# Held-back additions, a staggered start of v, and weights factored in rounds: a Strassen-Winograd attention kernel for two layers

## The chip, the cores and the metric

The kernel runs on one core of one Trainium2 chip. The metric is the device time of one execution in microseconds. Engines are named as the profile names them: PE (matmul; PEld is its weight load), DVE (vector), ACT (scalar), POOL (GpSimd) and SP (the engine whose queue issues most DMAs).

## The reference

x has the shape [8, 512, 32, 32], all in fp32. Two layers follow each other, both of the same form; 8 groups, 8 heads of 64 channels, S = 1024 tokens per image:

```python
xn  = group_norm(x, groups=8, eps=1e-5) * gamma + beta
q, k, v = Wq @ xn + bq, Wk @ xn + bk, Wv @ xn + bv        # 512 -> 512 each
p   = softmax(q_h^T k_h / sqrt(64))                        # per head h, 1024 x 1024
x   = x + Wo @ concat_h(p v_h) + bo                        # 512 -> 512
```

## The kernel before, in words

**Jobs and stages.** One image in one layer is a job; there are 16, in the order (image 0, layer 0), (1, 0), (0, 1), (1, 1), (2, 0) and so on, in pairs of images. The work alternates between an *attention* of job n and a *phase* n+1, which holds the projections between it and the next attention: V of job n+1, the output projection O of job n, then K and Q of job n+1.

**Attention** (class `Attention`, from L1025) has 64 steps: 8 groups (head pair, half of the queries) of 8 key chunks. A step makes scores on PE (L1046), exp on ACT into a buffer `e` (L1051), and two steps later values on PE (L1097) into `po`. The softmax sums are DVE additions (L1065, L1067), some done by an accumulating DMA of POOL (L1074) and a later addition (L1077). At a group's end ACT copies one half of `po` to `px` (L1118) and DVE adds the other (L1120), the sums are reduced (L1132), gathered by small DMAs of SP, inverted (L1159, L1160) and spread, and q is normalised (L1189). Other small tasks ("chores") are laid at fixed steps of an attention by `put`: the group norm of the next job (its last read-back is the DMA L324, then factors on DVE at L332 to L334, then xn on ACT at L339), sums of xn for the fast multiplication, and the making of weight factors.

**Projections** use the Strassen-Winograd scheme with 7 products for a 2 by 2 block product. K, Q and O are *deep*: two levels, 7 outer chains of 7 inner products, each one matmul of 128x128 on 128x256 (L758). V is one-level in jobs below `DEEP_V` = 3 (L522) and deep from there (L753, 128x128 by 128x128, two matmuls per product). Within a chain the seven products go in a fixed order (1, 5, 6, 2, 7, 3, 4) into PSUM banks named z, y, u, v; ACT copies an intermediate from bank to bank (L466, L470) or to a small buffer `s5` (L785), and the four results are *put*: by ACT (L765, L774, L776) or, for products 7 and 3, by DVE with an addition of `s5` (L781, L783). The seven chain results are then combined by DVE additions of 128x1024 (L797 for K and Q; `plus` at L808 and `add_five` at L803 for V; `more` at L831 for O). `deep_phases` (L602) writes this order: the list `at` interleaves two chains at a time, and for V's first two chains gives an order of its own.

**The order on DVE** is made on the host. Each emitted product advances a model clock; `pump` (L658) takes work from queues by `next_work` (L634): `values` (V's additions), `planned` (the sums that O's products need, with earliest time and due time), `outer` (K's, Q's, O's additions), `extra`. It takes work while DVE's modelled end is less than `AHEAD` = 0.8 us past the clock, and only if the duration (1.22 for an addition, 0.72 for a five-add) fits before the next put's time (`limits`, with `SLACK` = 1.3). An instruction once emitted is executed in that order on its engine.

**The end of an attention.** From job 2's attention on, the first two thunks of V's phase (2 products) are emitted ahead of the last values (`between` in `Attention.run`, L1195), a third between the copies of the two halves of `po` (`middle` in `take`, L1112).

**Weights.** Deep weights lie in device memory, one tile of 7 inner factors per (matrix, layer, outer factor), and are loaded ahead of use through a ring of 6 by SP. They are made on the chip: one-level factors by `first_factors` (L1321) in attentions 0, 1 and 2, in a buffer of tag "deep", stored by `store_factors` (L167); the second level for O, K and Q by `prepare` (L199) in the phase where a matrix is first used, as 28 DVE additions of 128x128 (L159 to L165 through `factor`, L156); for V by `deep_values` (L211) in attentions 2 and 3, in tiles taken from the pool of `e` buffers.

Of the kernel before, what the change touches and what calls it, by code (L numbers as in the profile page):

```python
# [50 lines left out]
AHEAD, TAIL, SLACK = 0.8, 12.0, 1.3  # L51
PLACE = {2: (0, 0), 6: (0, 1), 5: (1, 1), 7: (1, 0)}
DEEP_V = 3
# [25 lines left out]
def fast_path(  # L79
# [87 lines left out]
    def store_factors(w, layer, which):  # L167
        keep = wdram.tile([P, NW, 2, CH], F32, name=f"keep_{which}_{layer}")
        if (which, layer) == (O, 1):
            nc.sync.dma_start(keep, w)  # L170
        else:
            for s in (slice(S1, NW), slice(S3, S3 + 1)):
                nc.sync.dma_start(keep[:, s], w[:, s])
        factors[which, layer] = keep
# [36 lines left out]
    def deep_values(layer):  # L211


        box = {}

        def load(o):
            w = epool.tile([P, NW, P], F32, tag="e", name=f"w_values_{layer}_{o}")
            box[o] = w
            src = (
                raw_block(layer, V, *BLOCK[o]) if o in BLOCK else factors[V, layer][:, FACTOR[o]]  # L220
            )
            nc.sync.dma_start(wide(w), src)

        def make(o):
            w = box.pop(o)
            for part in range(4):
                factor(w, part)
            keep = wdram.tile([P, NW, P], F32, name=f"deep_{V}_{layer}_{o}")
            deep[V, layer, o] = keep
            later(1.0, lambda: nc.sync.dma_start(keep, w))  # L230

        return load, make
# [369 lines left out]
    def deep_phases(n, extra, outs=None, early=()):  # L602
# [11 lines left out]
        began, free_at = [], [0.0]  # L614
# [19 lines left out]
        def next_work(c, forced=False, limit=None):  # L634
            now = clock[0] - began[0] if began else 0.0
            room = 9.9 if limit is None else limit - max(free_at[0], clock[0])
            if planned and planned[0][1] <= now and not forced:
                _, _, _, us, fn = planned.popleft()
            elif values:
                if values[0][0] > room:  # L640
                    return False
# [3 lines left out]
            elif outer:  # L645
                if room < 1.22 and outer[0] not in free:
                    return False
# [14 lines left out]
        def plan_sums():  # L662
            start, combined = out_combines(n - 1, outs)
            c0, c1, c2, c3, c4, c5, c6 = (outs.steps(c) for c in range(7))
            later(0.1, c0[0])
            later(1.0, c0[1])
# [14 lines left out]
        fives = {}  # L681
# [6 lines left out]
        def begin(c):  # L688
# [24 lines left out]
            tiles[which, o] = e  # L713
            s5 = small.tile([P, QT], F32, tag="s5", name=f"s5_{n}_{c}", bufs=3)
# [4 lines left out]
            z, y, u, w = (bank(half, b, f"{b}d_{n}_{c}")[:, :QT] for b in names)  # L719
# [67 lines left out]
        def end(c):  # L787
# [7 lines left out]
            def add(to_, a, b, frees):  # L795
# [3 lines left out]

                outer.append(go)  # L800

            if which == V:
                def add_five():  # L803
                    to_ = p(o)[:, 2:4, :].rearrange("p t (o c) -> p t o c", o=2)
# [3 lines left out]
                def plus(to_, a):  # L808
# [3 lines left out]

                    values.append((1.22, go))

                if c < 2:
                    add_five()
                    spend(0.72)
                else:
                    values.append((0.72, add_five))
# [7 lines left out]
            if which == O:  # L827
# [3 lines left out]
                def more(oh, sh, part, moved=False):  # L831
# [19 lines left out]
                    waiting[oh, sh] += 1  # L851
                    if not moved:
# [78 lines left out]
        if with_v:  # L931
            at[:11] = [
                (0, 0), (0, 1), (0, 2), (0, 3), (0, 4), (1, 0), (0, 5), (1, 1), (0, 6), (1, 2), (1, 3)
            ]
# [90 lines left out]
    class Attention:  # L1025
# [101 lines left out]
        def reduce(self, g):  # L1127
# [63 lines left out]
            times = (0.0, 0.2, 2.0, 4.0) if ends else (0.0, 7.6, 7.7, 16.2)  # L1191
# [3 lines left out]
        def run(self, chores, between=None, middle=None):  # L1195
# [8 lines left out]
            for i in range(3, len(steps) + LEAD):  # L1204
                if i < len(steps):
                    self.scores(i)
                if i - LEAD == len(steps) - 1 and between:
                    between()
# [6 lines left out]
                if kc == NT - 1:  # L1215
                    if middle and g + 1 == len(self.groups):
                        self.reduce(g)
                        self.take(g, middle)
# [101 lines left out]

    def first_factors(put, which_layers):  # L1321

        box = []

        def start():
            box.append(acts.tile([P, 2, NW, 2, CH], F32, tag="deep", name=f"raw_{len(factors)}"))
            for i, (which, layer) in enumerate(which_layers):
                load_blocks(box[0][:, i], layer, which)

        put(2, start)  # L1330
# [543 lines left out]
```

## Time and profile before

| | us |
|---|---|
| median of 4 runs | 3254.39 (3253.22 to 3254.71) |
| the profiled execution | 3253.61 |
| its span | 3251.8 |
| PE busy | 3191.9 |
| DVE busy | 2672.5 |
| ACT busy | 2054.8 |
| POOL busy | 279.7 |

The profiled execution's own time is 1.8 us more than its span. The granted TensorE clock was 0.998. Stages, as they stand in the trace from the first matmul of one to the first matmul of the next:

| stage | us | stage | us |
|---|---|---|---|
| attention 0 | 110.12 | phase 1 | 92.46 |
| attention 1 | 110.03 | phase 2 | 92.91 |
| attention 2 | 116.45 | phase 3 | 96.16 |
| attention 3 | 112.20 | phase 4 | 91.19 |
| attention 4 and most later ones | 109.17 | most later phases | 90.6 |

A stage's length is read against that of a later stage with the same matmuls: attentions all have the same, phases 3 and later too (phases 1 and 2 have the one-level V). Idle time on an engine other than PE has a price only where PE waits for it in the end.

### The profile page before, as it was taken

To read this page: it belongs to the slowest core of one execution; us is meant where nothing else is said; L and a number is where in the kernel's file an instruction comes from. 1 tells how busy PE (TensorE), PEld (TensorE's weight loads), DVE (VectorE), ACT (ScalarE), POOL (GpSimd) and SP (SyncE) were. 2 spreads that over 40 slices of the span, in tenths; PEclk is the share of its full clock that TensorE was granted. 3 is DMA by queue.
4 is the path that set the end of the run, shared out by engine and by line. 5 is a ranking of instruction groups with operands and counts; after the bars stand their busy time and mean duration, and the time that the engine had idled before them with its cause. 6 is when DMAs were issued, how large, how long until landed. Compare 5 with 4: busy or idle time off the path is not lost.

```text
span 3251.8 us, 61327 instructions
## 1 busy us (share of the span) xinstructions
PE 3191.9 (98%) x24009; PEld 1862.2 (57%) x24009; DVE 2672.5 (82%) x3952; ACT 2054.8 (63%) x3583; POOL 279.7 (9%) x318
## 2 busy tenths in 40 slices
PE   9999999999999999999999999999999999999998
PEld 7365483563846638365483754737557374573844
DVE  8796897979879788796987969789697896978957
ACT  4746656566666666666666666666666666666663
POOL 0100001001010010100001000010000100001000
PEclk9999999999999999999999999999999999999999
DMA  7555556667635354455554535446455463544733
GB/s 270 139 148 135 148 178 152 179 171 182 203 73 147 104 143 129 86 160 141 138 174 93 166 86 134 119 93 187 121 134 173 90 196 61 139 113 98 212 85 78
DMA packets 188810, 453.47 MB, mean 139 GB/s; under 512 B 38120, under 2 KB 56160, under 8 KB 188256
## 3 DMA queue, kind: packets, MB, share of 16 engines
q1 hardware_dynamic: 139664, 300.04, 27.9%
q0 software_dynamic: 48848, 149.44, 25.1%
q8 instruction: 190, 3.11, 0.4%
q14 instruction: 108, 0.88, 0.1%
HBM read 246.69 MB, written 52.10 MB: 92 GB/s over the span
## 4 chain that ended last, share of the span: by engine, by line
PE 82%; DVE 11%; DMA 4%; issue 2%; ACT 1%; SPq 0%; POOL 0%; DVEq 0%; ACTq 0%; POOLq 0%
PE sc L1046 25%; PE po L1097 25%; PE zd L758 8%; PE vd L758 8%; PE yd L758 3%; PE vd L753 3%; PE ud L758 3%; PE zd L753 3%; DVE acc L1067 1%; PE ud L753 1%; PE yd L753 1%; DMA x<-p 1%; DMA w<-deep 1%; DVE k L797 1%; PE z L522 1%
## 5 line engine op out<-in xcount | busy, mean ns | idle before, releaser
L1051 ACT ACTIVATE e<-sc 128x1024 f32<-128x1024 f32 x1024 | 1043.0, 1023 | 574.0 <-PE sc L1046 521.0
L1046 PE MATMUL sc<-q,k 64*64 64x512 f32 x8192 | 1059.4, 590 | 8.7 <-ACT e L1051 8.4
L1097 PE MATMUL po<-e,v 64*64 64x512 f32 x8192 | 1061.0, 590 | 0.0
L1046 PEld LDWEIGHTS sc<-q,k 64*64 64x64 f32 x8192 | 311.0, 133 | 574.0 <-issue 514.1
L1097 PEld LDWEIGHTS po<-e,v 64*64 64x64 f32 x8192 | 312.0, 133 | 560.9 <-issue 546.0
L1067 DVE TENSOR_TENSOR acc<-acc,e 128x1024 f32<-128x1024 f32 x320 | 389.2, 1216 | 49.9 <-ACT e L1051 41.7
L1074 POOL DMA_DIRECT2D e<-e x224 | 192.2, 858 | 1749.3 <-ACT e L1051 1272.0
L1065 DVE TENSOR_TENSOR acc<-e,e 128x1024 f32<-128x1024 f32 x128 | 156.3, 1221 | 202.4 <-ACT e L1051 202.3
L1077 DVE TENSOR_TENSOR acc<-acc,e 128x1024 f32<-128x1024 f32 x224 | 272.1, 1215 | 1.9
L758 PE MATMUL zd<-deep,w 128*128 128x256 f32 x860 | 245.0, 384 | 22.7 <-DVE p L783 20.7
L758 PE MATMUL vd<-deep,w 128*128 128x256 f32 x804 | 224.5, 380 | 3.4 <-ACT yd L466 1.6
L758 PEld LDWEIGHTS zd<-deep,w 128*128 128x128 f32 x860 | 159.0, 190 | 59.0 <-DVE p L783 31.5
L758 PEld LDWEIGHTS vd<-deep,w 128*128 128x128 f32 x804 | 152.2, 190 | 26.4 <-ACT yd L466 2.0
L1132 DVE TRANSPOSE_TENSOR_REDUCE r<-acc 128x32 f32<-128x1024 f32 x128 | 159.4, 1245 | 4.3
L839 POOL DMA_DIRECT2D x<-p x61 | 72.9, 1195 | 1003.0 <-ACT p L774 621.3
L785 ACT COPY s<-vd 128x256 f32<-128x256 f32 x195 | 72.6, 372 | 114.7 <-PE vd L758 63.4
L785 ACT COPY s<-zd 128x256 f32<-128x256 f32 x209 | 77.8, 372 | 102.3 <-PE zd L758 57.9
L1120 DVE TENSOR_TENSOR q<-po,px 128x512 f32<-128x512 f32 x115 | 78.3, 681 | 49.0 <-ACT px L1118 48.9
L470 ACT COPY ud<-vd 128x256 f32<-128x256 f32 x209 | 75.2, 360 | 64.7 <-PE vd L758 53.5
L470 ACT COPY ud<-zd 128x256 f32<-128x256 f32 x195 | 71.0, 364 | 70.5 <-PE zd L758 43.2
L753 PE MATMUL vd<-w,deep 128*128 128x128 f32 x780 | 113.1, 278 | 0.0
L758 PE MATMUL vd<-os,w 128*128 128x256 f32 x368 | 109.6, 387 | 2.1 <-DVE p L783 0.6
(308 smaller groups left out, 4717.4 us busy)
## 6 DMA issues: line engine op xcount, KB each, us to landing
w<-deep SPq DMA_DIRECT2D x378, 448.0 KB, 5.5
e<-e POOLq DMA_DIRECT2D x224, 512.0 KB, 4.7
x<-p POOLq DMA_DIRECT2D x61, 512.0 KB, 7.6
rb<-rd SPq DMA_DIRECT2D x96, 256.0 KB, 4.0
deep<-w SPq DMA_DIRECT2D x42, 448.0 KB, 3.6
x<-x_dram SPq DMA_DIRECT2D x28, 512.0 KB, 3.7
out_dram<-x SPq DMA_DIRECT2D x28, 512.0 KB, 3.2
w<-keep SPq DMA_DIRECT2D x32, 256.0 KB, 4.8
```

Source lines behind the costliest of these rows:

```text
L470: nc.scalar.copy(u, z)
L753: nc.tensor.matmul(ps[:, tokens], moving[i][:, tokens], lhs[:, FACTOR[i], :], start=(start and ti == 0), stop=True, skip_group_check=True,)
L758: nc.tensor.matmul(ps, lhs[:, FACTOR[i], :], moving[i], start=start, stop=True, skip_group_check=True,)
L785: return chain(product, lambda ps: nc.scalar.copy(s5, ps), put, z, y, u, w)
L1046: nc.tensor.matmul(sc[h * HD : (h + 1) * HD, j, :], k[r, hp, k0 : k0 + HD], q[r, hp, sh * HALF : (sh + 1) * HALF], start=True, stop=True,)
L1051: nc.scalar.activation(e, sc, AF.Exp, scale=SCALE)
L1065: nc.vector.tensor_add(acc[g], self.es[i - 1], e)
L1067: nc.vector.tensor_add(acc[g], acc[g], e)
L1074: nc.gpsimd.dma_start(self.summed[i], self.summed.pop(i - 1), accum_op=ALU.add)
L1077: nc.vector.tensor_add(self.acc[g], self.acc[g], self.summed.pop(i))
L1097: nc.tensor.matmul(po[g][j * HD : (j + 1) * HD, h, :], v[r, kc, d0 : d0 + HD], e[r, j, :], start=(kc == 0), stop=(kc == NT - 1),)
L1132: nc.vector.tensor_reduce(self.r[:, 0, m, :], self.acc.pop(g).rearrange("p j (b e) -> p (j b) e", e=RP), AX.X, ALU.add, apply_transpose=True,)
```

## The change

**Additions are queued later.** Each addition gets a time before which the planner does not take it: the model clock at the end of the product chain that makes its last term, plus `BEHIND` = 1.2 us. It holds for K, Q, O and V alike. V's five-adds, which free an `s5`, are forced when two more chains have begun.

**V's start.** The last values of an attention come first, then the copy px, V's first product, and the copy py; V's first two chains are interleaved product by product from their third product on. The PSUM banks of a chain are allocated in the order y, u, v, z whatever their use. The first sums for O are emitted at 6.2 and 6.9 us instead of 0.1 and 1.0, the spread of the last group's inverse 5.6 us later than before and its normalisation 4.2 us later.

**Weights.** V is deep from job 2. `first_factors` and `deep_values` go. `deep_round` makes both levels of one matrix in one buffer [128, 7, 7, 128]: 4 loads of 256 KB, 4 DVE additions of 128x512, 4 of 128x896, and one store of 3136 KB. Two rounds run in each of attentions 0 and 1 (from steps 2 and 25), one in attentions 2 and 3; they use the same buffer tag one after the other. Layer 0's K and Q stay as before. The deep steps of attention 1 are put at steps 49 to 58, and layer 1's output bias is made in phase 2 from the queue `ahead`.

```diff
-AHEAD, TAIL, SLACK = 0.8, 12.0, 1.3
+AHEAD, TAIL, SLACK, BEHIND = 0.8, 12.0, 1.3, 1.2
-DEEP_V = 3
+DEEP_V = 2
+ROUNDS = {0: ((O, 0), (K, 1)), 1: ((V, 1), (Q, 1)), 2: ((O, 1),), 3: ((V, 0),)}
...
+    def deep_round(which, layer):
+        box = []
+        def start():
+            t = acts.tile([P, NW, NW, P], F32, tag="deep", name=f"round_{which}_{layer}")
+            box.append(t)
+            for i in range(2):
+                for j in range(2):
+                    nc.sync.dma_start(
+                        t[:, 2 * j + i, 0:4, :].rearrange("p (cc h) o -> p cc (h o)", cc=2),
+                        raw_block(layer, which, i, j),
+                    )
+        def outer_(part):
+            factor(box[0][:, :, 0:4, :], part)
...
+        def inner(part):
+            factor(box[0].rearrange("p f a o -> p a f o"), part)
+        def store():
+            keep = wdram.tile([P, NW, NW, P], F32, name=f"deep_{which}_{layer}")
+            nc.sync.dma_start(keep, box[0])
...
         def next_work(c, forced=False, limit=None):
             now = clock[0] - began[0] if began else 0.0
-            room = 9.9 if limit is None else limit - max(free_at[0], clock[0])
+            start = max(free_at[0], clock[0])
+            room = 9.9 if limit is None else limit - start
+            if forced:
+                start = 1e9
...
-                if values[0][0] > room:
+                if values[0][0] > room or ready[values[0][1]] > start:
                     return False
...
-                if room < 1.22 and outer[0] not in free:
+                if outer[0] not in free and (room < 1.22 or ready.get(outer[0], 0.0) > start):
                     return False
...
-            later(0.1, c0[0])
-            later(1.0, c0[1])
+            later(6.2, c0[0])
+            later(6.9, c0[1])
...
+            while unread and unread[0] <= c - 3:
+                next_work(c, True)
...
-            z, y, u, w = (bank(half, b, f"{b}d_{n}_{c}")[:, :QT] for b in names)
+            taken = {b: bank(half, b, f"{b}d_{n}_{c}")[:, :QT] for b in sorted(names, key="yuvz".index)}
+            z, y, u, w = (taken[b] for b in names)
...
+                ready[go] = clock[0] + BEHIND
                 outer.append(go)
...
-                (0, 0), (0, 1), (0, 2), (0, 3), (0, 4), (1, 0), (0, 5), (1, 1), (0, 6), (1, 2), (1, 3)
+                (0, 0), (0, 1), (1, 0), (0, 2), (1, 1), (0, 3), (1, 2), (0, 4), (0, 5), (1, 3), (0, 6)
...
-            times = (0.0, 0.2, 2.0, 4.0) if ends else (0.0, 7.6, 7.7, 16.2)
+            times = (0.0, 0.2, 7.6, 8.2) if ends else (0.0, 7.6, 7.7, 16.2)
...
-                if i - LEAD == len(steps) - 1 and between:
-                    between()
                 self.values(i - LEAD)
...
-                    if middle and g + 1 == len(self.groups):
+                    if taken and g + 1 == len(self.groups):
                         self.reduce(g)
-                        self.take(g, middle)
...
-                if n == 0:
-                    first_factors(put, [(O, 0), (V, 1)])
-                elif n == 1:
-                    first_factors(put, [(K, 1), (Q, 1)])
-                elif n == 2:
-                    first_factors(put, [(O, 1)])
+                for at, made in zip((2, 25), ROUNDS.get(n, ())):
+                    first, *made, store = deep_round(*made)
+                    put(at, first)
+                    for i, fn in enumerate(made):
+                        put(at + 4 + i, fn)
+                    put(at + 12, store)
...
+                    late = (49, 50, 51, 53, 54, 55, 57, 58)
+                    for at, fn in zip(late if n == 1 else (41, 43, 45, 47, 49, 51, 53, 55), deep_first):
...
-                if DEEP_V - 1 <= n <= DEEP_V:
-                    load, make = deep_values(jobs[n + 1][1])
-                    for i, o in enumerate(OUTER_V):
-                        put(23 + 4 * i, lambda o=o: load(o))
-                        put(29 + 4 * i, lambda o=o: make(o))
...
-                att.run(chores, between, both[2])
+                att.run(chores, True)
                 extra = ahead
                 plan_sums()
-                banks(1, "one")
+                banks(0, "one")
                 if n + 2 < len(jobs):
                     reads, steps = norm_steps(n + 2)
-                for thunk in both[3:]:
+                att.take(len(att.groups) - 1, both[0])
+                banks(1, "one")
+                for thunk in both[1:]:
                     thunk()
```

## Prediction

> **What bounds the kernel.** I read the page's busy line first, then the slices, the costliest groups, a table of windows by stage, the waits, and then the timeline around each wait.
>
> ```profile
> span 3251.8 us, 61327 instructions
> PE 3191.9 (98%) x24009; PEld 1862.2 (57%) x24009; DVE 2672.5 (82%) x3952; ACT 2054.8 (63%) x3583; POOL 279.7 (9%) x318
> ```
>
> PE is busy 98% of the span at a granted clock of 0.998, so a change can win in two ways only: fewer or shorter matmuls, and fewer gaps between them. The windows (columns: stretch, its us, busy time and count of PE, PEld, DVE, ACT, POOL, clock, DMA share, GB/s) say where the gaps are. They are attention 1, attention 2, phase 3, attention 3, a steady phase and a steady attention:
>
> ```profile
> 285.00:395.00 110.00, 110.00 (x1025) 38.97 (x1024) 86.73 (x107) 73.00 (x76) 12.63 (x15) 1.00 0.59 138
> 490.00:604.00 114.00, 108.74 (x1000) 37.82 (x992) 93.72 (x134) 71.31 (x75) 12.78 (x15) 0.99 0.67 173
> 604.00:700.50 96.50, 90.27 (x506) 76.99 (x498) 80.90 (x151) 57.60 (x156) 5.99 (x5) 1.00 0.64 195
> 700.50:812.50 112.00, 109.43 (x1017) 38.56 (x1016) 94.65 (x137) 73.17 (x76) 12.61 (x15) 1.00 0.62 150
> 1013.00:1104.00 91.00, 89.31 (x506) 77.59 (x506) 76.56 (x125) 57.49 (x157) 4.77 (x4) 1.00 0.47 137
> 1104.00:1212.70 108.70, 108.70 (x1016) 38.55 (x1008) 88.65 (x109) 73.16 (x76) 12.62 (x15) 1.00 0.49 107
> ```
>
> Measured from first matmul to first matmul in the trace, a steady attention lasts 109.17 us and a steady phase 90.60; but attention 2 lasts 116.45 (7.3 more), attention 3 112.20 (3.0 more) and phase 3 96.16 (5.6 more). Phases 1 and 2 last 92.46 and 92.91. The rest repeats at 199.8 us per job, and its loss sits in the phase, where matmul starts 0.2156 us apart (128x256) and 0.1113 (128x128) would make 86.1 us, 4.5 less than the 90.6.
>
> **The change, part by part.** All sums are against the profiled run, 3253.61 us (span 3251.8, 1.8 around it); the median of the runs, 3254.39, is 0.8 above it.
>
> *1. Attention 2, V's weights.* There ACT's exp waits for the store of a small weight tile, since those tiles are taken from the buffers that exp writes, and PE waits in turn:
>
> ```profile
> PE sc L1046 <- ACT e L1051: 5.3, 2, 3.7
> ACT e L1051 <- DMA deep<-w_values: 9.4, 2, 5.7
> ```
>
> The change makes V's factors in a buffer of their own (the tag "deep", free in early attentions). These two waits end, and the restarts after them; of the 7.3 us about 1 may remain, since DVE is the busiest here (93.7 of 114): **-6.5** (bounds -7.3 and -5, the latter if DVE is late next). Attention 3 likewise: **-2.7** of 3.0 (bounds -3.0 and -1).
>
> *2. Prepares out of the phases.* In phase 1 (O, layer 0), 2 (K, Q, layer 1) and 3 (O, layer 1) DVE makes each product's inner factors between the adds: 28 instructions of 128x128 per matrix at 282 to 292 ns, 8.0 us each. DVE's puts and adds are what PE waits for in phase 3 (five waits of 0.4 to 0.8 us on L783 or L781, three of 0.4 to 1.4 on ACT's copy L470, one of 0.7 on a load). Without them phase 3 becomes a steady phase: -5.6, and -0.4 for part of what 4 gains: **-6.0** (bounds -7 and -4). In phase 1 DVE is 67.7 of 81 us busy and V stays one-level: its stalls are only 4.9 us over the spacing, and I take the prepares' part, **-1.8** (bounds -3 and 0). Phase 2 gets the deep V: 196 matmuls at 0.1113 are 21.8 us in place of 112 at 0.2156, 24.1, so -2.3; and of its 5.4 us of stalls some 0.6 go: **-2.9** (bounds -4 and -1).
>
> *3. The rounds' price, attentions 0 and 1.* A round adds, on DVE, four 128x512 (0.68 each) and four 128x896 instructions (not in the trace; between 128x768 at 0.95 and 128x1024 at 1.22, so 1.08): 7 us, 14 for two, less 5.3 of removed factors. DVE goes from 86.7 to about 100 of 110 in attention 1, which also takes the deep steps of V: full, not over. What weighs more is SP's queue. The round's result leaves as one store of 3136 KB, and the second round's first load waits at SP's head for it, with everything behind it. In attention 1 that is the group norm's read-back:
>
> ```profile
> 307.63 1.86 SPq L324 DMA_DIRECT2D mr<-dg  x2
> 318.87 0.15 DVE L332 TENSOR_TENSOR mul<-mr,vec_sb 128x4 f32<-128x4 f32 x1
> 324.96 1.23 ACT L339 ACTIVATE xn<-x,off,mul 128x1024 f32<-128x1024 f32 x1
> ```
>
> Before, mr is issued at 307.63, lands 6.4 us later, and ACT uses it at 324.96 with nothing to wait for. After, the store is issued near 311.5. Its duration isn't in the trace: the tile view of the existing factor stores gives 7.4 us for 1792 KB, which by size makes 12.9, an upper end; the fastest slice of the DMA view (463 GB/s) makes 7, the lower. I take 12.9, since the 1792 KB store is the nearest row. Then mr is issued near 325, lands near 330, and ACT, which has exp of later scores queued behind xn, stands about 6 us; scores run less than one step (1.72) ahead, so PE loses some 5 to 6, and DVE's wait for mr delays the sums whose buffers exp needs: **+6** (at 7 us for the store 0, at 12.9 with DVE pushed over its slack 12). This row speaks against the change. The Trainium skill, "DMA: Bandwidth & Descriptors", section on the anatomy of one DMA, fits a DMA as 2.0 us plus bytes over 436 GB/s, 9.4 us by estimate here; with it the wait would be about 2.5 instead of 6. "Perfetto Trace Analysis", section DMA Optimizations, says that splitting DMAs may let some start sooner: a rule against the single store, which no row of before can test. In attention 0 the same block delays a gather by some 4 us; DVE has 110.5 - 85.9 = 25 us of room, less the 9 added: **+1** (bounds 0 and 3).
>
> *4. Steady phases, 12 of them (4 to 15).* (a) V's start: two products begin ahead of attention's last values.
>
> ```profile
> 1212.94 0.71 PE L753 MATMUL vd<-w,xn 128*128 128x128 f32 x4
> 1214.03 1.09 PE L1097 MATMUL po<-e,v 64*64 64x512 f32 x8
> 1215.05 0.71 PE L753 MATMUL vd<-w,deep 128*128 128x128 f32 x4
> 1215.19 0.59 ACT L1118 COPY px<-po 128x512 f32<-128x512 f32 x1 [0.68 <-PE po L1097]
> ```
>
> PE changes tile shape three times; I count some 1.0 us over the spacing here, of which 0.3 (one change) must stay. The change puts the values first and lets two products alternate after them. ACT must then do px, py (0.59 each) and the products' copies (0.36) within the first products; walking ACT's copies at these durations against matmuls at 0.1113 leaves about 0.1 of stalls beside the one change of shape, since the first products use the banks (v, z) that are free early: 0.4 in place of 1.0, **-0.6** (ends -0.7 and, if the crowd on ACT holds PE for a whole px, 0). (b) Inside V, the product's third buffer (s5, three of them) waits for a five-add that is queued behind other adds; 0.15 to 0.7 plus 0.26 per phase. The forced service two products later takes about **-0.3**. (c) K's and Q's ends. This is the page's dearest idle of a phase, 20.7 us in all, two of 0.79 per phase:
>
> ```profile
> L758 PE MATMUL zd<-deep,w 128*128 128x256 f32 x860 | 245.0, 384 | 22.7 <-DVE p L783 20.7
> ...
> 1076.27 2.49 DVE L797 TENSOR_TENSOR k<-k 128x1024 f32<-128x1024 f32 x2 [0.84 <-ACT k L774]
> 1078.68 0.48 DVE L783 SCALAR_TENSOR_TENSOR p<-zd,bias_step,s 128x256 f32<-128x256 f32 x1
> 1079.21 0.70 PE L758 MATMUL zd<-deep,w 128*128 128x256 f32 x2 [0.79 <-DVE p L783]
> ```
>
> The first add was queued 0.84 before its term was there; two adds (2.49) then make the put 1.5 late where about 0.5 is free, so PE waits (0.97 with the restart). The change holds an add back for 1.2 us after its product's last step. At Q's end the adds then come behind the put: -1.07. At K's end one add lies between the puts of the next product and pushes by about 1.4: -0.1 only. In O the held-back adds meet the sums' blocks of four (1.5 us) and the puts are later there: +1.3 by my walk through the order of DVE's instructions. (c) is **+0.1**, with -2 and +2.5 as ends. Per phase -0.6 - 0.3 + 0.1 = -0.8; twelve make **-9.6** (ends -24 and +20).
>
> Sum: -6.5 - 2.7 - 6.0 - 1.8 - 2.9 + 6 + 1 - 9.6 = -22.5, so **3231 us**.
>
> **Rivals.** *A: waits only change places.* (c) plus ACT's crowded start of V cancel (a) and (b): 12 x 0.8 = 9.6 given back, 3241. For it: ACT and DVE serve PE step by step with 0.5 us of slack. *B: both ends' gaps vanish*, with no loss in O: 12 x 1.2 less again, about 3217. For it: the cause of each 0.79 gap is an add queued too early. Against it: the K end, where the window between two puts (3.0 us) holds the later adds too. *C: slower.* The held-back adds bunch: where three adds (3 x 1.14 to 1.22, 3.4 to 3.7) fall between two puts 3.0 us apart, of which the puts themselves take 0.8 and about 0.5 is free, the put is late by 0.7 to 1.0 and by more at the next. With the early gains standing (-13), it decides from +1.1 us per phase over 12; at +2 it gives 3253.6 - 13 + 24 = 3265. Against it: DVE is 76.6 of 91 us busy in a phase, so backlogs drain. *D: SP blocked worse.* The stores cost 12 in attention 1 and 3 in attention 0 instead of 7: 3239. *E: staged weights aren't there in time*, so that phases 1 and 2 wait for their first loads; unlikely, as the stores land 60 us ahead.
>
> **How the numbers follow.** Forecast (3224 to 3236) 0.40, A and D together 0.27, B 0.17, C 0.10, E or another way of no gain 0.06. A measurement of this kernel can tell about 0.2%, 6.5 us, from no change. Faster by more than that: forecast, B and nearly all of A and D, 0.83; within it 0.08; slower 0.09. The range leaves out C and the last of B and E: 3212 to 3249, narrower than the ends of 4 alone since those twelve phases can't all be at an end without a whole window of adds going wrong.
>
> **What the changed profile would show.** Right: in attentions 2 and 3 no wait of exp on a store, lengths near 109.5; phase 3 near 91; one gap near 0.8 per phase on L783's counterpart instead of two; no values among V's first matmuls; in attention 1 ACT's xn waiting for DVE's factors near 40 us into it, PE's scores for exp behind it, 5 us or so. Wrong: a phase as long as 90.6 or longer (A, C); the 0.8 gaps all gone (B); attention 1 longer than 116 (D) or 110 (store faster than its row says).

## The result, and the profile after

The changed kernel takes 3258.68 us (median of 40 runs, 3253.55 to 3267.81) beside 3254.56 us for the kernel before (60 runs): ratio 1.0013, 95% interval 1.0009 to 1.0018. It is 4 us slower than before; the forecast was 3231, in a range of 3212 to 3249. The profiled execution took 3260.8 us. First the top of its page:

```profile
span 3259.0 us, 61423 instructions
PE 3187.3 (98%) x24093; PEld 1861.8 (57%) x24093; DVE 2662.0 (82%) x3822; ACT 2093.7 (64%) x3623; POOL 280.6 (9%) x318
```

PE is busy 4.6 us less than before and the span is 7.2 longer: the waits grew. The stages, from first matmul to first matmul, say where. (Before, from attention 2 on, two of V's products and the last values stood in each other's stage; to compare like with like, 0.86 us, eight of the values' matmul records, is moved there from the phase to the attention.)

| stage | before | after | difference |
|---|---|---|---|
| up to attention 0 | 82.47 | 83.22 | +0.8 |
| attention 0 | 110.12 | 117.63 | +7.5 |
| phase 1 | 92.46 | 88.62 | -3.8 |
| attention 1 | 110.03 | 128.73 | +18.7 |
| phase 2 | 92.91 | 88.09 | -4.8 |
| attention 2 | 117.31 | 122.22 | +4.9 |
| phase 3 | 95.30 | 88.30 | -7.0 |
| attention 3 | 113.06 | 120.25 | +7.2 |
| phase 4 | 90.33 | 89.69 | -0.6 |
| attention 4 to phase 15 | 2203.25 | 2190.61 | -12.6 |
| the rest | 144.56 | 141.64 | -2.9 |

So every phase gained, all but phase 4 (0.6 for 0.8) more than forecast, and the four attentions with rounds lost 38 us. In the windows by stage (attentions 1, 2, 3, a steady phase and a steady attention; columns as in the prediction) the losing stages also show something that no stage of before did, a granted clock below 0.98:

```profile
289.50:418.20 128.70, 117.92 (x1025) 38.96 (x1024) 100.85 (x120) 73.23 (x76) 13.44 (x15) 0.93 0.62 163
506.30:628.50 122.20, 112.86 (x1025) 38.13 (x1024) 97.64 (x121) 73.35 (x76) 13.13 (x15) 0.96 0.58 149
716.80:837.00 120.20, 112.50 (x1025) 38.06 (x1024) 97.67 (x121) 73.35 (x76) 13.15 (x15) 0.96 0.55 137
1036.80:1125.00 88.20, 86.79 (x494) 77.03 (x490) 72.87 (x121) 59.26 (x156) 4.77 (x4) 1.00 0.49 135
926.80:1036.70 109.90, 109.90 (x1025) 39.01 (x1024) 91.47 (x113) 73.33 (x76) 12.55 (x15) 1.00 0.50 111
```

The small transfers have these names in the rows below. For the group norm, `dm` takes the statistics of x out and `gm` brings them back by groups, `dg` takes the groups' factors out and `mr` is their read-back. For the softmax sums, `r` is the gather, `rd` takes the inverse out and `rb` spreads it.

**Attention 2**, from its waits: DVE stands 8.6 us for the gathered group statistics, ACT's xn waits for DVE, the scores wait for ACT's exp.

```profile
ACT xn L352 <- DVE off L347: 10.3, 1, 10.3
...
PE sc L1071 <- ACT e L1076: 9.3, 1, 9.3
DVE gs L327 <- DMA gm<-dm: 8.6, 1, 8.6
```

SP's timeline shows the statistics leaving only at 545.33, behind both stores of the round; before, in the same attention, they left at 499.17, 11 us into it (first line; the others are of the changed kernel).

```profile
499.17 1.93 SPq L303 DMA_DIRECT2D dm<-mv  x2
...
533.83 0.34 SPq L239 DMA_DIRECT2D deep<-round  x1
542.63 2.65 SPq L1180 DMA_DIRECT2D r<-r  x3
545.33 2.79 SPq L316 DMA_DIRECT2D dm<-mv  x2
551.42 0.32 SPq L320 DMA_DIRECT2D gm<-dm  x1
```

The lateness is DVE's first, not SP's: its statistics of x end at 544.0. `put` moves a chore to the next free step. The rounds are put first, on steps 2 and 6 to 14; nine pieces of the norm, which an attention without a round has on steps 3 to 11, go to 3, 4, 5 and 15 to 20, and the reading of the groups goes from 18 to 21. One step (1.7 us) is left for a round trip through two DMAs (8.4 us here from the first issue to the use).

**After the stall** PE runs slowly for a while; one line is a group of eight 64x512 matmuls:

```profile
563.92 1.98 PE L1071 MATMUL sc<-q,k 64*64 64x512 f32 x8 [9.34 <-ACT e L1076]
565.69 1.93 PE L1122 MATMUL po<-e,v 64*64 64x512 f32 x8
567.39 1.93 PE L1071 MATMUL sc<-q,k 64*64 64x512 f32 x8
569.10 1.11 PE L1122 MATMUL po<-e,v 64*64 64x512 f32 x8
570.04 1.03 PE L1071 MATMUL sc<-q,k 64*64 64x512 f32 x8
```

The granted clock is 0.50 from 563.9 to 567.9, and three groups take 1.93 to 1.98 in place of 1.03; by the matmuls' starts that is 2.6 us more on top of the gap.

**Attention 1** loses most at its end. The second round's store leaves at 361.24; `rd`, issued behind it, holds `rb` until 374.27, DVE uses `rb` 9.3 us later, and the additions that free exp's buffers come late.

```profile
361.24 0.35 SPq L239 DMA_DIRECT2D deep<-round  x1
366.25 0.33 SPq L1197 DMA_DIRECT2D rd<-rt  x1
374.27 1.30 SPq L1199 DMA_DIRECT2D rb<-rd  x2
...
383.60 1.23 DVE L1214 TENSOR_TENSOR q<-q,rb 128x1024 f32<-128x1024 f32 x1 [6.95 <-DMA rb<-rd]
```

**The phases.** V's start is now one change of shape, with the copy px beside the first products, and the end-of-Q gap is gone (the page's row of before that had 22.7 us idle has 1.2; the gap at K's end is left and now stands in the row of `vd`):

```profile
1036.77 0.71 PE L772 MATMUL vd<-w,xn 128*128 128x128 f32 x4
1036.91 0.59 ACT L1143 COPY px<-po 128x512 f32<-128x512 f32 x1 [1.55 <-PE po L1122]
...
1037.32 0.61 PE L772 MATMUL zd<-w,deep 128*128 128x128 f32 x4
```
```profile
L777 PE MATMUL zd<-deep,w 128*128 128x256 f32 x860 | 240.9, 379 | 1.2 <-DVE p L800 0.6
L777 PE MATMUL vd<-deep,w 128*128 128x256 f32 x804 | 227.7, 381 | 9.4 <-DVE p L802 7.5
```

### The profile page after: what moved, and what is told of

Its sections match the earlier page's. It is cut to its first block, busy times and chain, and to the rows that moved or that the text cites. A ratio compares the mean times of both kernels' runs of the same rounds, so it can differ in the third digit from the quotient of the medians.

```text
span 3259.0 us, 61423 instructions
## 1 busy us (share of the span) xinstructions
PE 3187.3 (98%) x24093; PEld 1861.8 (57%) x24093; DVE 2662.0 (82%) x3822; ACT 2093.7 (64%) x3623; POOL 280.6 (9%) x318
## 4 chain that ended last, share of the span: by engine, by line
PE 69%; DVE 3%; DMA 3%; issue 1%; SPq 0%; ACT 0%; DVEq 0%; POOLq 0%
PE sc L1071 21%; PE po L1122 21%; PE zd L777 7%; PE vd L777 7%; PE vd L772 3%; PE yd L777 3%; PE ud L777 3%; PE zd L772 3%; DMA x<-p 1%; PE yd L772 1%; PE ud L772 1%; DMA w<-deep 1%; DVE v L831 0%; DVE q L430 0%; DVE p L800 0%
```

## The experiments

The theory after the first look: the two planner parts are worth about 1.4 us per job; the rounds cost it all back because their chores displace the norm. The rivals: the single store of 3136 KB; too many additions for DVE. All times are medians; the ratio is to the kernel before, with its interval.

**The planner's parts.** *e1* has the later additions alone (weights and V's start as before):

```diff
+                ready[go] = clock[0] + BEHIND
...
+            while unread and unread[0] <= c - 3:
+                next_work(c, True)
```

> The kernel before with the later additions alone (BEHIND, and the five-adds forced after two chains); weights and V's start as before. Theory 1, the parts are separate: Q's end loses its 0.8 us gap (1.07 with the restart), K's keeps it, V's inner waits shrink by 0.3 to 0.5, O gains about 0.75 of waits: the steady phase of 90.6 us becomes about 89.9, and 13 such phases make -9 us, about 3245. Rival: the later additions need the new start of V to pay (the queue that they wait in is filled at the start): the phase stays within 0.3 of 90.6 and the time within 3 us of before.

3254.6, ratio 0.9996 (0.9986 to 1.0006). *e2* has the new start alone:

```diff
-AHEAD, TAIL, SLACK = 0.8, 12.0, 1.3
+AHEAD, TAIL, SLACK, BEHIND = 0.8, 12.0, 1.3, -99.0
...
-                (0, 0), (0, 1), (0, 2), (0, 3), (0, 4), (1, 0), (0, 5), (1, 1), (0, 6), (1, 2), (1, 3)
+                (0, 0), (0, 1), (1, 0), (0, 2), (1, 1), (0, 3), (1, 2), (0, 4), (0, 5), (1, 3), (0, 6)
```

> The new start of V with the other order of banks, later first sums, and forced five-adds, but additions never held back (BEHIND = -99); weights as before. Theory 1: the three changes of tile shape at V's start become one, -0.7 us per job, with both 0.8 us gaps (K's and Q's end) still there; attention plus phase go from 199.8 to about 199.1, in all -9, about 3245. Rival: the copies of po, now on ACT together with the first products' copies, give the gain back: 199.8, 3254.

3251.35, ratio 0.9991 (0.9981 to 1.0). *e3* has both, `BEHIND` = 1.2, with before's weights:

> Both together, that is everything of the change but the weights (V deep from job 3, factors as before). Theory 1: the steady job is the changed kernel's, 198.3 us, attentions 0 to 3 are those of before (110.1, 110.0, 116 to 117, 112 to 113), phase 3 about 1.5 to 2.5 shorter than before's: 13 jobs x 1.45 = -19, about 3236. Then the weights' rounds cost the changed kernel +23. Rival: the gain of the phases comes in part from the rounds (weights that are there earlier): the steady job stays above 198.9 and the time above 3243.

3239.02, ratio 0.9951 (0.9934 to 0.9967): faster than both kernels. The parts do not add. Time over the matmuls' own spacing in one steady phase, read from PE's starts:

| | V's start | O and sums | end of K | end of Q | one job |
|---|---|---|---|---|---|
| before | 1.0 | 1.2 | 1.07 | 1.08 | 199.77 |
| later additions (e1) | 1.0 | 2.3 | 0.86 | 0 | 199.58 |
| new start (e2) | 0.3 | 2.0 | 1.07 | 1.08 | 199.60 |
| both (e3, and the changed kernel) | 0.3 | 2.0 | 0.86 | 0 | 198.33 |

Each part by itself pays in O nearly what it gains elsewhere (in e1 one put of O is some 1.6 us late). With both, O's loss is the 0.8 of the new start alone, and not the sum of the two; why was not tested. Theory 1 had 90.6 to 89.9 for e1 alone and missed the size of O's loss; e1's rival, a time within 3 us of before, is what came.

**The weights' part alone**, *e7*:

> The kernel before with the weights' part of the change alone (rounds, V deep from job 2), no later additions, V's start as before. If the parts add up, it costs what the changed kernel has more than the run without the rounds: 3258.7 - 3239.0 = +20, about 3275, with attentions 0 to 3 near 118, 129, 122, 120 and steady jobs of 199.8. Rival: with the old start of V the gains of phases 1 to 3 differ; then anything from 3262 on.

3275.69, ratio 1.0067 (1.005 to 1.0084): +20 us beside its own runs of before, as the sum had it. The profiled run was the fastest of its four (3269.23); its attentions 0 to 3 take 118.3, 122.7, 120.2 and 118.3, so attention 1 shows less there than the 129 expected.

**What in the rounds costs.** *e4* puts the norm's chores first, the rounds' pieces on what is left:

```diff
-                for at, made in zip((2, 25), ROUNDS.get(n, ())):
...
                 for i, fn in zip(at, steps + sums(n + 1)):
                     put(i, fn)
+                for at, made in zip((2, 25), ROUNDS.get(n, ())):
```

> The changed kernel, with the steps of an attention given first to the group norm and the sums of xn, and the rounds' pieces put on the steps left over; the same work, the same single stores. Theory 1: in attentions 2 and 3 the rounds' eight additions had pushed the norm's statistics from steps 3 to 11 to steps 3 to 20, right before the step that reads the groups back, so DVE waited 8.6 and 8.0 us for gm: both attentions fall from 122.2 and 120.3 to about 110.5, attention 1 loses its first stall (6.7 us) or half of it: -22 to -28, 3231 to 3237. Rival 2, the single store of 3136 KB: whatever the order, SP's queue and the DMA engines are held for 10 us and the norm's small transfers land late: attentions 2 and 3 shorten by under 5 us each, attention 1 stays near 128. Rival 3, too many additions for DVE: the stalls move to other waits (sums, rb) and the four attentions together keep most of their excess of 49 us.

3259.62: nothing gained in all; theory 1 fell as a single cause. Attentions 0 to 3 take 118.7, 120.5, 123.5, 125.2: attention 1 gained 8 us, the other three lost 1 to 5. The displacement is gone and another wait stands in its place, here in attention 2:

```profile
539.12 2.06 SPq L239 DMA_DIRECT2D deep<-round  x1
541.53 2.29 SPq L337 DMA_DIRECT2D mr<-dg  x2
545.84 0.33 SPq L1197 DMA_DIRECT2D rd<-rt  x1
556.99 1.27 SPq L1199 DMA_DIRECT2D rb<-rd  x2
```
```profile
556.90 0.16 DVE L345 TENSOR_TENSOR mul<-mr,vec_sb 128x4 f32<-128x4 f32 x1 [7.85 <-DMA mr<-dg]
```

The 2 KB read-back issued 2.4 us after the store is used 15.4 us later; the 8 KB of rd take 11 us where before's median is 1.5. *e5* issues the store from POOL's queue:

```diff
-            nc.sync.dma_start(keep, box[0])
+            nc.gpsimd.dma_start(keep, box[0])
```

> The run with the norm first (attentions 0 to 3: 118.7, 120.5, 123.5, 125.2 us), with the rounds' single stores issued from POOL's queue instead of SP's; everything else equal. There the read-back mr was issued 2.4 us behind a store and landed 15.4 us later. Theory A, a queue carries out its DMAs in order: with the store in another queue mr and the small transfers of the softmax sums land in 2 to 6 us, attentions 2 and 3 fall to about 110.5 to 113, total -20 to -28 (3232 to 3239). Theory B, the 16 DMA engines themselves are taken up for 10 us, whichever queue the store came from: attentions 2 and 3 stay above 118, the total within 6 us of 3259.6.

3262.2. mr lands 10.7 to 11.0 us after its issue in attention 2, from another queue than the store: most of the delay is not the queue's order (4 us of the 15 went). That is as theory B has it; that the shared part is the DMA engines is argued, not shown. Attention 0 became longer, 131.5: there rd and rb are late beside the first store, and DVE stands 11.8 us for rb. *e6* stores in seven pieces, in attentions 1 to 3:

```diff
-                    put(at + 12, store)
+                    for i, fn in enumerate(store):
+                        put(at + 12 + i, fn)
```

> Norm first in attentions 1 to 3 as before, and each round's store there in seven pieces of 448 KB, one per free step (1.7 us or more apart); attention 0 as in the changed kernel. By theories A and B alike a small transfer then stands behind one or two pieces (3.6 us each by before's rows) instead of 10 us: attentions 2 and 3 to 110.5 to 113, attention 1 to 112 to 118, total about 3235. Rival, DVE: the additions themselves are too many for attentions 1 to 3 (97.6 and 100.9 of 110 us busy), so the stalls stay at half or more: 3245 or above.

3259.23, not what was wanted from the edit: SP stood behind another wait, and all seven pieces left within 539 to 550, as one store would. It says nothing on spreading. *e9* takes the bytes away instead:

```diff
-            nc.sync.dma_start(keep, box[0])
+            nc.sync.dma_start(keep[:, 0], box[0][:, 0])
             for o in OUTER:
-                deep[which, layer, o] = keep[:, FACTOR[o]]
+                deep[which, layer, o] = keep[:, 0]
```

> The changed kernel with one seventh of each round's store (448 KB of 3136); all deep weights of these matrices are then read from that one factor, so values are wrong while all transfers of the phases keep their sizes. Chores displaced and all additions stay. If the stores are the cause, attentions 0 to 3 (117.6, 128.7, 122.2, 120.3) fall to 110 to 112 and the time to about 3225. If the displaced chores are (attentions 2 and 3, where the groups are read one step after they are gathered), these two keep 118 or more, and only attentions 0 and 1 shorten: about 3240 to 3245. If DVE's additions are, little changes in all four: above 3250.

> The run with the norm first (118.7, 120.5, 123.5, 125.2) with one seventh of each round's store; otherwise as the last. Without displaced chores and without the big stores only DVE's additions and the loads are left. If store and displacement are the two causes, all four attentions come to 110 to 112 and the time to about 3222. If DVE is overbooked, stalls remain near the ends of attentions 1 to 3, where the deep sums stand: 114 to 118 each, about 3238.

With the chores as in the change (e9): 3241.8, attentions 115.6, 112.5, 121.1, 119.6. With the norm first (e10): 3228.99, ratio 0.9916 (0.99 to 0.9933), attentions 110.7, 110.6, 115.4, 115.4. So in attention 1 taking the store's bytes away is nearly enough (-16), and in 0, 2 and 3 *either* cause alone keeps most of the stall: one takes the other's place. Some 5 us are left in 2 and 3. *e11* leaves out additions:

```diff
+        apart = (which, layer) in ((O, 1), (V, 0))
...
-            factor(box[0][:, :, 0:4, :], part)
+            if not apart:
+                factor(box[0][:, :, 0:4, :], part)
```

> The run with the norm first, leaving out the eight DVE additions of each round of attentions 2 and 3 (7 us of DVE each); the parts of the buffer that they would have written are filled by more loads at the round's begin (768 KB and 1344 KB), so values are wrong, and the full single stores stay, issued earlier, as nothing is waited for. Attentions 0 and 1 unchanged. If DVE's additions cause the stalls, attentions 2 and 3 (123.5, 125.2) fall to 110 to 112; if the store, they stay at 116 or above, or fall only because the store now precedes the norm's read-back by more: then mr lands within 6 us of its issue.

3244.24; attentions 2 and 3 at 118.4 and 113.3, from 123.5 and 125.2 with the norm first: neither reading came out whole. The store, ready earlier, now hits the gather (dm issued at 520.5, gm only at 535.75). The additions alone are not the cause, but they decide what the store meets.

**Laying the same bytes elsewhere.** *e13* and *e14*:

```diff
-                for at, made in zip((2, 25), ROUNDS.get(n, ())):
+                for at, made in zip(((2, 12, 19 if n < 2 else 23, 27), (28, 35, 39, 44)), ROUNDS.get(n, ())):
                     first, *made, store = deep_round(*made)
-                    put(at, first)
+                    put(at[0], first)
                     for i, fn in enumerate(made):
-                        put(at + 4 + i, fn)
-                    put(at + 12, store)
+                        put(at[1 + i // 4] + i % 4, fn)
+                    put(at[3], store)
```

> The changed kernel, complete, with the same rounds laid round the norm and the sums: norm's steps first; a round's first four additions after the norm's gather, the last four only after the norm's read-back and the first spread, so that the single store of 3136 KB becomes ready there and SP issues it behind mr, rd and rb; the second rounds of attentions 0 and 1 from step 28. If the stores hurt by when they run (and not by their bytes), attentions 0 to 3 come to 110 to 113 and the time to 3222 to 3232. If bytes or DVE's additions are the price wherever they stand, attentions stay at 117 and above and the time above 3245.

> The same layout with one seventh of each store, the deep weights all read from that factor (wrong values, same transfers in the phases). It shows what of the last run's loss is the big store: if the layout is quiet, it equals the last run within 3 us; attentions 2 and 3 show whether the 5 us left with the norm first and short stores (115.4 each) were the additions standing ahead of the group statistics (now 110 to 111) or something else (115 again).

e13, with all bytes: 3241.33, ratio 0.9956 (0.9939 to 0.9972). Attentions 2 and 3 are quiet, with the full store, the same additions on DVE, and full clock:

```profile
507.20:617.80 110.60, 110.19 (x1025) 38.94 (x1024) 97.26 (x121) 73.18 (x76) 12.54 (x15) 1.00 0.64 162
706.20:816.80 110.60, 110.18 (x1025) 38.90 (x1024) 97.44 (x121) 73.17 (x76) 12.61 (x15) 1.00 0.60 149
```

In these two attentions it is when the store runs, not its bytes, and 97 of 110 us of DVE is not too much. The 5 us left in e10 went too (110.67 in e14). e14 takes 3220.4: attentions 0 and 1 at 110.6 and 111.8 against 124.0 and 123.5 in e13, so there it is still the store. Its trace names the second one: DVE's deep sums, which write the same buffer, wait 7.9 and 4.5 us for it at the ends of the two attentions. The expectation that e13 and e14 agree within 3 us failed for that. *e15* moves the second rounds earlier, two additions to a step:

```diff
-..., (28, 35, 39, 44)), ROUNDS.get(n, ())):
+..., (28, 39, 43, 46)), ROUNDS.get(n, ())):
```

> The last complete layout, with the second rounds of attentions 0 and 1 done by step 45 (their additions two to a step from step 39), so that their stores are issued near steps 45 and 46, behind the second spread and ten steps before the third gather; in the last run they were issued at steps 55 and 50, just before it. If the time of the store decides, attentions 0 and 1 fall from 124.0 and 123.5 to 111 to 113, with 2 and 3 still at 110.7: 3217 to 3222. If it is the bytes and DVE's load of these two attentions, they stay above 117 and the time above 3230.

3239.18; attentions 0 and 1 still 121.6 and 126.7. Here too the deep sums wait to write the buffer that the store is still reading, 4.0 us in attention 0 and 6.4 in attention 1,

```profile
186.01 0.96 DVE L464 TENSOR_TENSOR deep<-t 128x768 f32<-128x768 f32 x1 [4.00 <-DMA deep<-round]
```

and DVE, late by that, holds the sums that free exp's buffers (exp waits 11.0 and 10.5 us for DVE's additions). Neither layout serves two rounds in one attention.

**Better versions.** Two were tried on e3's own stalls in attentions 2 and 3 (118.8 and 114.2, exp waiting 8.6 us for V's small stores). *e8* makes V's factors in the buffer "deep", *e12* issues those stores from POOL:

```diff
-            w = epool.tile([P, NW, P], F32, tag="e", name=f"w_values_{layer}_{o}")
+            t = acts.tile([P, NW, NW, P], F32, tag="deep", name=f"values_{layer}")
...
-            later(1.0, lambda: nc.sync.dma_start(keep, w))
+            later(1.0, lambda: nc.gpsimd.dma_start(keep, w))
```

> The run with both planner parts and before's weights (3239.0), with one edit: V's inner factors are no longer made in tiles out of exp's buffers, but in the buffer of tag deep, from the stored one-level factors, by four 128x896 additions, stored in seven pieces two to a step, behind the norm's steps. Theory: attentions 2 and 3 were longer there (118.8 and 114.2 against 110.0) because exp waited for those tiles' stores: both go to 110 to 111.5: -10 to -12, 3227 to 3230. Rival: the stalls come from DVE or the transfers and not from the buffers: under 4 us gained, 3235 or above.

> The run with both planner parts and before's weights (3239.0; attentions 2 and 3 at 118.8 and 114.2), with the stores of V's small weight tiles issued from POOL's queue instead of SP's. If exp waits because these stores stand behind SP's waits for other things, attentions 2 and 3 fall to 110 to 113: -5 to -11, about 3230. If the store's own time or DVE's lateness holds the buffers, under 3 us.

3245.18 and 3242.56, ratios 0.997 (0.9959 to 0.9982) and 0.9958 (0.9941 to 0.9974) beside e3's 0.9951: neither is faster than e3. In e8 attention 2 takes 131.5 (DVE waits 10.5 us for rb, and its deep sums 6.3 us for the last store) and attention 3 gains 2 us. In e12 exp waits for the accumulating DMAs instead in attention 2 (10.1 us) and for the same small stores as before in attention 3 (5.7). *e16* keeps one round per attention in the quiet layout with `DEEP_V` = 3, and *e17* the same with `DEEP_V` = 2:

```diff
-ROUNDS = {0: ((O, 0), (K, 1)), 1: ((V, 1), (Q, 1)), 2: ((O, 1),), 3: ((V, 0),)}
+ROUNDS = {0: ((V, 1),), 2: ((O, 1),), 3: ((V, 0),)}
...
+                if n == 0:
+                    first_factors(put, [(O, 0)], 28)
+                if n == 1:
+                    first_factors(put, [(K, 1), (Q, 1)])
```

> A complete kernel that keeps both planner parts and at most one round per attention, in the quiet layout: V of layer 1 in attention 0, O of layer 1 in attention 2, V of layer 0 in attention 3; O of layer 0 and K, Q of layer 1 are factored and prepared as in the kernel before, and V is deep from job 3. From the run without rounds (3239.0: attentions 118.8 and 114.2, phase 3 93.6): attentions 2 and 3 at 110.7, phase 3 at 88.3, attention 0 up by at most 3: -16, about 3223. If a single round in attention 0 already brings back a stall of 10 us (its store, or the deep buffer that its deep sums wait for), about 3233.

3222.55, ratio 0.9895 (0.9878 to 0.9911); but in this kernel V of job 2 took one block of its weights from the finished factors, where it is overwritten, so only its time counts. *e17* is complete:

> As the last run (3222.6), where V of job 2 took its one-level weights from the finished deep factors, of which one block is overwritten, so that it was computed with a wrong block; here V is deep from job 2, as in the change, which needs no one-level factors of V, and the kernel is complete. K and Q of layer 1 are still prepared in phase 2, now beside a deep V: that phase about 93 (88.1 in the changed kernel, where they come from rounds); attentions 0 to 3 at 110 to 111.5, phase 1 near 92.4. In all 3218 to 3226. If the 56 prepares of 0.28 us in phase 2 hold V's additions up, phase 2 goes to 98 and the time to 3230.

3224.54, ratio 0.9902 (0.9886 to 0.9919): 32 us faster than its own runs of before and 34 faster than the change. Attentions 0 to 3 take 113.6, 112.5, 110.7, 110.7 in the profiled run; the first two are above the 110 to 111.5 expected. Phase 2, with the prepares of K and Q, takes 97.1, near the 98 of the rival, though the time stayed in the forecast.

## Why the prediction was wrong, point by point

1. *V's weights, attentions 2 and 3* (-6.5 and -2.7). This is the step that failed: +4.9 and +7.2, so 9 us of forecast gain came out as 12 of loss. That the waits on the small stores end was right. But the sum had no term for the round that comes in their place in these two attentions: it was put at nothing, without a reason. A round's DVE time and its store were priced for attentions 0 and 1 only, and that `put` would shift the norm's statistics behind the round's additions was overlooked. What the runs showed in its place: the displaced norm alone keeps the stall (e9, 121.1 and 119.6), the store beside the norm's small transfers alone keeps it (e4, 123.5 and 125.2), without both 115.4 is left (e10), and with the additions behind the statistics 110.7 (e14).
2. *Prepares out of the phases* (-1.8, -2.9, -6.0). Right in kind and too small: -3.8, -4.8, -7.0. Phase 1's gain is the weights' alone: it takes 88.7 in e7, which has the rounds and not the planner's parts, and 92.4 in e3, which has those and no rounds. So more of the stalls of phases 1 and 2 went with the prepares than the working had put down to them.
3. *The rounds' price, attentions 0 and 1* (+1 and +6). Failed in size: +7.5 and +18.7. In attention 0 the block came as described (the gather r left at 123.57 in place of 119.71), and DVE stood 6.5 us for it. Not foreseen was that DVE then had the second round's eight additions (141.4 to 154.2) ahead of the norm's factors, for which ACT's xn waited 6.2 us:

```profile
156.63 0.16 DVE L345 TENSOR_TENSOR mul<-mr,vec_sb 128x4 f32<-128x4 f32 x1
...
157.22 1.24 ACT L352 ACTIVATE xn<-x,off,mul 128x1024 f32<-128x1024 f32 x1 [6.19 <-DVE off L347]
```

   The first stall of attention 1 was as described (SP issued the round's load at 324.88, mr at 325.30, ACT's xn late): 4.1 us of gap and 2.9 of slow clock. Two things were missed: the group reading itself was displaced (steps 10 to 15: dg left at 319.75 instead of 306.47), so the store was only the last of mr's delays; and the *second* store, for which no price was set, made rd (8 us) and rb (9.3) of the sums late, for 12 us more at the attention's end. "Full, not over" for DVE was right only without such waits.
   The store's own duration was right by luck. The 7.4 us that the working reads as that of a 1792 KB store is in the trace of before that of a 256 KB load:

```profile
443.95 7.45 DMA w<-keep
```

   No row of before has the duration of a store of that size, so nothing on record carries the term of 12.9 us. What the changed kernel shows are 10.0 and 11.7 us for the two stores of 3136 KB whose landing its trace has. The 9.4 of the Trainium skill ("DMA: Bandwidth & Descriptors", section on the anatomy of one DMA) was an estimate by a fit that the page gives for DMAs issued by GpSimd; this store is SP's, and both figures miss.
4. *Steady phases* (-9.6). Right in direction and too small: -13.2 in attention 4 to phase 15 and phase 4; the one steady job is 1.44 shorter where 0.8 was said. (a) -0.7 as worked out (-0.6); (b) -0.15 (-0.3); (c) -0.5 instead of +0.1: Q's gap went, K's stayed at 0.76 as described, and O lost 0.8, not 1.3. The walk charged this to the held-back additions; alone (e1) they cost O 1.1, but the new start alone (e2) costs the same 0.8 without them.

Of the rivals, B's time needed all gaps gone and A and C spoke of the phases; that C's 3265 is near the measured time is chance, since no phase became longer. None had attentions 2 and 3 turn. D had the mechanism for attentions 0 and 1, at 8 us more where it was 19 (26.2 there instead of 7), and its sign, attention 1 longer than 116, was seen.

Open: attention 9 of the changed kernel is 4.3 us longer than its neighbours, in most kernels that have rounds (111.4 to 114.4; not in e5, e7 and e17) and in none of e1, e3 and before; there the gather r takes 7.4 us. And the 2.9 us gained after the last attention began were not looked into.

## What to carry to other kernels

A chore put into a full schedule costs the place of what it pushes away: list what moved, and read for each the round trip that it must still fit. A store of megabytes is not paid in bytes but in the small transfers that land while it runs, so lay it where none is due, and remember who writes its source next. Two sufficient causes for one stall hide each other: remove them one at a time and together (attentions 0, 2 and 3 of this kernel changed by +7 us in all without the displacement, by -4 without the store's bytes, by -19 without both).

## What the runs showed of the hardware

- In the traces of all the runs, every PE gap of 3.9 to 12 us ahead of an attention's scores was followed by half clock (0.50 granted, 1.93 for 1.03 us), and where no second gap came soon, that cost 1.3 to 2.9 us more. The Trainium skill, "TensorE: Matmul & The Clock Gate", section on why this matters for kernels, warns of PE-idle gaps over about 3 us. The traces agree: by the matmuls' starts in the changed kernel a gap of 9.7 us cost 2.6 more and one of 4.1 cost 2.9. Shorter ones differ: one of 2.6 (attention 9) cost 1.7, one of 3.4 (e12, at 598) nothing. The prediction's "restarts" had no number for it.
- POOL's small power for the norm (8x1) takes 0.56 us in a quiet attention and 3.44 in e10, where DVE runs three additions without a pause (518.86 to 522.08), two of them the round's:

```profile
519.07 3.44 POOL L332 TENSOR_TENSOR ga<-gv,neg_half 8x1 f32<-8x1 f32 x1 [11.32 <-issue]
522.47 1.48 POOL L1099 DMA_DIRECT2D e<-e  x2
```

  The Trainium skill, "SBUF — State Buffer", section on the two separate sides, says that a DVE operation with two SBUF inputs and a GpSimd operation that reads SBUF exclude each other for a whole instruction. The row agrees in kind, though it spans three instructions; no run tests that cause by itself. In e10 SP issues dg only after this power (522.54), and the last part of the sums' gather behind it (522.89). With the additions moved behind the power (e14) it takes 0.57 us, and attentions 2 and 3 lost their last 5 us.
- While a 3136 KB store ran, transfers of 2 to 8 KB took 4.7 to 15 us, mostly 8 or more, issued from the store's queue or from another (without it, in before, medians of 1.5 us for rd, 4.4 for mr and 5.6 for dm). POOL's 512 KB accumulating DMAs issued close to the store took 13.3 to 14.5 us (median of all 4.6).
